# Two small table stores per batch, issued by ScalarE instead of SyncE

## The chip, the cores and the metric

The kernel runs on one core of one Trainium2 chip. A core has five engines with an instruction queue each: TensorE (PE, matmuls), VectorE (DVE), ScalarE (ACT), GpSimd (POOL) and SyncE (SP, which here does nothing but issue transfers). All work through their queues in order and wait for each other by semaphores. Transfers between the on-chip memory and HBM run on 16 DMA engines; here SP issues nearly all of them, POOL the indexed ones, and ACT three tiny ones at the start. The metric is device time in microseconds: the median of several runs. A profile is one further execution.

## The reference

Two layers of a graph network on `x` of 32 batches x 512 channels x 1024 nodes, each with a residual and a layer norm:

```python
# layer 0, per batch
q = einsum('c,cn->n', wq, x);  k = einsum('c,cn->n', wk, x)
scores = leaky_relu(q[None, :] + k[:, None], 0.01)
att = softmax(scores, axis=-1)
agg = einsum('cn,mn->cm', x, att)
x = layernorm(x + relu(einsum('oc,cm->om', adj, agg) + bm[:, None]), axis=-1)
# layer 1, per batch
x = layernorm(x + einsum('nf,nm->mf', x, adj * adj) + bias, axis=-1)
```

Layer 0's weight is `adj`, layer 1's `support * kernel` with both equal to `adj`.

## The kernel before

**Attention without the 1024 x 1024 matrix.** A score depends on q[n] + k[m] alone, and leaky ReLU has two branches, so exp(score) is a product of a factor in n and a factor in m on either side of a threshold. With the nodes sorted by q, the sum over n for a given m is a prefix sum with one factor plus a suffix sum with the other. For each batch the kernel therefore

- projects x to rows of 512 values and an attention column (`project`, L338, PE; `keep`, L357 and L359, DVE and ACT copies out of PSUM);
- ranks the nodes by q (`place`, L403, DVE) and counts for each m how many lie under its threshold (`count`, L428, ACT, after `line`, L395, has copied q);
- scatters the rows to a table in HBM in order of rank (`send`, L415, POOL), and fetches them back sorted into nine blocks `zs` (`fetch`, L461 and L466, SP);
- makes the table of prefix and suffix sums in nine steps (below);
- gathers for each m its rows of the table (`pick`, L543, POOL), scales and adds them (`scale`, `gain`, L582 and L587), transposes (`turn`, L596) and normalises: `add` L603 on DVE, `square` L611 and L612 on ACT, `root0` L619 and L620 on POOL, `finish` L627 and L628 on ACT.

Layer 1 follows with seven half-size products instead of eight (`multiply`, L676, on PE, out of `y`), `read` (L699, L697), statistics, `apply` (L729) and `store` (L734).

**A table step.** Step k (0 to 8) handles block 8 - k from one end (the suffix sums, i = 0) and block k from the other (the prefix sums, i = 1):

- `t{k}`: eight matmuls on PE with triangular weights (L510), four for each block;
- `e{k}`: ACT copies both results out of PSUM (L522); from step 4 on they overwrite blocks of `zs`;
- `cp{k}` and `ca{k}`: the last row of each result is carried into the next block (L528), for i = 0 by POOL, for i = 1 by ACT. `t{k+1}` needs both;
- `ts{k}` (`table_store`, L530 to L539): two stores of 60 rows x 2052 bytes (48 rows for the last block) to the table in HBM, i = 0 first.

```python
        for i, j in enumerate(blocks(step)):
            n = RH if j < NB - 1 else TL
            nc.sync.dma_start(
```

Here NB is 9, RH 60 and TL 48. Step 7's second store is of 60 rows, step 8's of 48.

**The order.** It is written out by hand. Three strings of step names say in which order work is issued: `BEGIN` (batches 0 and 1 and what belongs beside them), `SLOT`, which is run 28 times and interleaves four neighbouring batches, and `END`. Every engine gets its instructions in that order. `SLOT` handles the table of batches 2 to 29. Around the last two table steps it reads:

```python
    ... t7 p27 e7 ld2 mx cp7 ts7 k121 qb mr ca7 rt2 en ts4 y1 t8 r0 sA e8 r1
    sB sq3 ts8 m0 sh sd0 ql ld3 T1 m1 c0 sd1 r2 m3 rdp1 pi3 r3 y2 m2 rt3 r4 pi2 y3 m6 ...
```

On ACT this gives `e7`, `k121` (L359), `ca7` (L528), `y1` (L627 and L628), `e8`, `sq3` (L611, L612), `ql` (L395), `c0` (L428), `rdp1` (L699), `y2`, `y3` (L627 and L628 each). `p27`, `mx`, `qb`, `t8` and `m6` are PE's. In `m6` PE reads what `y3` has written. POOL has `sd0` and `sd1` (scatters of the next batch), then `pi3`, the first gather, which waits for all 18 stores of the table, and behind it `rt3`, the root that `y3` needs.

**Transfers and semaphores.** Transfers of SP and ACT share eight semaphores, handed out in turn in the order of the program. A transfer waits, before it is issued, for the landing of the one that had its semaphore before, eight places earlier. For `ts7`'s second store that is `ld0`, a load of 512 KB of x (L131); for `ts8`'s second store it is `ts6`'s first. A store also waits for the copy that wrote its source.

Of the kernel before, what the change touches and what calls it, by code (L numbers as in the profile page):

```python
# [23 lines left out]
def gat_gcn_resnorm_kernel(  # L24
# [11 lines left out]
    nc = tc.nc  # L36
# [13 lines left out]
    NB = N // R + 1  # L50
# [449 lines left out]
    def blocks(step):  # L500
        return NB - 1 - step, step
# [28 lines left out]
    def table_store(b, step):  # L530

        ts = tss[b, step]
        td = tdb[b % 2].rearrange("(s w u) c -> s w u c", w=2, u=3)
        for i, j in enumerate(blocks(step)):
            n = RH if j < NB - 1 else TL
            nc.sync.dma_start(
                out=td[j * RH : j * RH + n, 0, 1 + i, 1:ZW],
                in_=ts[i * G + 1 : i * G + 1 + n, 0 : ZW - 1],
            )  # L539
# [253 lines left out]
    for k in range(NB):  # L793
        also(1, f"t{k}", table, k)
        also(1, f"e{k}", table_out, k)
        if k < NB - 1:
            also(1, f"cp{k}", carry, k, 0, nc.gpsimd)
            also(1, f"ca{k}", carry, k, 1, nc.scalar)
        also(1, f"ts{k}", table_store, k)
# [177 lines left out]
```

## Time and profile before

| | |
|---|---|
| median of 3 runs | 2201.99 us (2200.96 to 2205.12) |
| the profiled execution | 2198.41 us, span 2196.7 us |
| PE, DVE, ACT, POOL busy | 96%, 81%, 75%, 45% of the span |
| mean granted clock of TensorE | 0.990 |
| stores of L536 | 576 of 120 KB or 96 KB, all issued by SP |
| one period of `SLOT` | about 65 us |

In a line of the order of time the first number is the start in us from the span's start, the second the length; a bracket names idle time of the engine before it and what ended it. In a line of busy time by stage the columns are the stretch and its length in us, then busy time and number of instructions of PE, PE's weight loads, DVE, ACT and POOL, the clock, the share of the DMA engines' time and GB/s. Issues of transfers stand under SPq or ACTq with the time that the queue took to issue them; what the engine itself does meanwhile is not shown by that line. PE's busy time is that of pipelined matmuls, whose ends are modelled.

### The profile page before, as it was taken

Reading aid. Unit: us, or ns where it says so; the run is one execution under the profiler, and the core shown is the slowest. Engines: PE = TensorE matmul, PEld = TensorE weight load, DVE = VectorE, ACT = ScalarE, POOL = GpSimd, SP = SyncE. Lnnn points to the kernel's source line nnn. Section 1 sums busy time; section 2 is a strip of 40 time slices with the busy share of each in tenths; the row PEclk is TensorE's granted clock in tenths of the full one; section 3 lists DMA queues with packets and bytes.
Section 4 is the critical chain, followed back from the end, with each engine's and each line's share of the span. In section 5 each row is a group of like instructions: output and inputs, shape, how many; then the busy total and the mean of one; then the engine's idle time right before and its main releaser. Section 6 shows DMA issues by size and latency. Waiting matters only on the chain.

```text
span 2196.7 us, 35479 instructions
## 1 busy us (share of the span) xinstructions
PE 2102.5 (96%) x11697; PEld 1222.4 (56%) x11697; DVE 1775.9 (81%) x3576; ACT 1652.8 (75%) x2758; POOL 987.6 (45%) x1291
## 2 busy tenths in 40 slices
PE   7879999999999999999999999999999999999877
PEld 5446555556555556555656555556655556655433
DVE  7567888888888888888888898888888888888666
ACT  1577777887777887777888777878777788777765
POOL 1344455444445444445443445544445544445442
PEclk9999999999999999999999999999999999999998
DMA  7567888878888777888777889887888887888752
GB/s 250 166 229 252 264 266 281 257 239 254 268 260 277 262 247 244 268 246 286 266 250 234 265 253 282 273 249 233 262 265 267 282 252 236 258 265 264 221 205 96
DMA packets 179152, 548.86 MB, mean 250 GB/s; under 512 B 27404, under 2 KB 27416, under 8 KB 178968
## 3 DMA queue, kind: packets, MB, share of 16 engines
q1 hardware_dynamic: 121600, 277.06, 43.7%
q0 software_dynamic: 57344, 269.52, 34.3%
q8 instruction: 93, 1.52, 0.3%
q14 instruction: 91, 0.75, 0.1%
q10 hardware_dynamic: 24, 0.01, 0.0%
HBM read 338.17 MB, written 208.30 MB: 249 GB/s over the span
## 4 chain that ended last, share of the span: by engine, by line
PE 62%; ACT 12%; DVE 10%; issue 6%; DMA 6%; POOL 3%; SPq 1%; DVEq 0%; POOLq 0%; ACTq 0%
PE zp_A L338 18%; PE tp L510 10%; PE oA L676 9%; PE zp_B L338 8%; PE op L596 5%; PE zp_C L338 4%; DVE junk L403 4%; ACT y L628 4%; PE oB L676 3%; PE oC L676 3%; DMA zs<-td 2%; ACT rows L582 2%; ACT v L699 1%; POOL zs L528 1%; DMA td<-zs 1%
## 5 line engine op out<-in xcount | busy, mean ns | idle before, releaser
L587 DVE SCALAR_TENSOR_TENSOR rows<-rows,ra 128x512 f32<-128x512 f32 x512 | 366.2, 739 | 20.9 <-ACT rows L582 17.6
L676 PE MATMUL oA<-y,adj_sb 128*128 128x512 f32 x768 | 356.6, 607 | 9.8 <-ACT y L628 6.3
L415 POOL DMA_INDIRECT td<-zrow,ranki x256 | 269.3, 1052 | 213.7 <-DVE idx L439 80.0
L510 PE MATMUL tp<-zs,lq 128*64 128x257 f32 x2304 | 335.1, 392 | 27.2 <-POOL zs L528 16.3
L543 POOL DMA_INDIRECT rows<-td,idx x256 | 297.1, 1160 | 88.1 <-issue 68.0
L403 DVE SCALAR_TENSOR_TENSOR junk<-qb,zrow,first 128x1024 int8<-128x1024 f32 x240 | 307.1, 1279 | 10.9 <-PE qb L376 4.2
L528 POOL COPY zs<-ts 1x513 f32<-1x513 f32 x128 | 93.2, 728 | 474.4 <-ACT ts L522 474.3
L338 PE MATMUL zp_A<-wb,x 128*64 128x257 f32 (+1 forms) x1536 | 278.9, 388 | 12.6 <-issue 3.5
L428 ACT ACTIVATE junk<-lq,kc 128x1024 int8<-128x1024 f32 x240 | 274.4, 1143 | 2.0
L603 DVE SCALAR_TENSOR_TENSOR y<-op,nbm,x 128x1024 f32<-128x1024 f32 x128 | 163.8, 1282 | 127.4 <-PE op L596 127.2
L676 PEld LDWEIGHTS oA<-y,adj_sb 128*128 128x128 f32 x768 | 144.7, 193 | 191.7 <-issue 153.8
L510 PEld LDWEIGHTS tp<-zs,lq 128*64 128x64 f32 x2304 | 168.7, 136 | 135.6 <-POOL zs L528 37.8
L582 ACT ACTIVATE rows<-rows,ra 128x512 f32<-128x512 f32 x256 | 180.1, 718 | 77.5 <-DVE den L574 39.5
L359 ACT COPY zrow<-zp_A 128x514 f32<-128x514 f32 x192 | 112.8, 588 | 147.4 <-PE zp_A L338 130.1
L338 PEld LDWEIGHTS zp_A<-wb,x 128*64 128x64 f32 (+1 forms) x1536 | 177.0, 155 | 77.3 <-issue 25.1
L528 POOL COPY zs<-zs 1x513 f32<-1x513 f32 x128 | 78.3, 611 | 253.0 <-ACT zs L522 253.0
L628 ACT ACTIVATE y<-y,nb,r 128x1024 f32<-128x1024 f32 x128 | 158.9, 1241 | 4.3
L705 DVE BATCH_NORM_STATS2 st<-v 128x6 f32<-128x512 f32 x240 | 151.9, 674 | 0.0
L612 ACT ACTIVATE x<-y,nm 128x1024 f32<-128x1024 f32 x128 | 147.2, 1150 | 4.2
L729 ACT ACTIVATE v<-v,nb,rs 128x1024 f32<-128x1024 f32 x120 | 148.1, 1234 | 2.3 <-DVE nb L721 1.4
L596 PE MATMUL op<-ident,rows 128*128 128x128 f32 x1024 | 141.2, 282 | 4.6 <-DVE rows L587 2.6
L596 PEld LDWEIGHTS op<-ident,rows 128*128 128x128 f32 x1024 | 114.9, 143 | 46.1 <-issue 24.6
(162 smaller groups left out, 3784.6 us busy)
## 6 DMA issues: line engine op xcount, KB each, us to landing
x<-in_x_dram SPq DMA_DIRECT2D x128, 512.0 KB
out_dram<-v SPq DMA_DIRECT2D x120, 512.0 KB
zs<-td SPq DMA_DIRECT2D x64, 602.3 KB
td<-zs SPq DMA_DIRECT2D x288, 120.2 KB
td<-ts SPq DMA_DIRECT2D x224, 120.2 KB
zs<-td SPq DMA_DIRECT2D x64, 240.9 KB
zs<-td SPq DMA_DIRECT2D x96, 120.5 KB
td<-zs SPq DMA_DIRECT2D x8, 514.0 KB
```

The costliest lines, as they stand in the source:

```text
L338: nc.tensor.matmul(zp[n : n + wide, m, 0:CE], side(b, g, a)[:, c, m * P + n : m * P + n + wide], wb[:, w, c, :], start=first and c == 0, s ...
L403: nc.vector.scalar_tensor_tensor(junk(b)[:, 0:N], qbs[b], zrow[:, nt, 0:1], first[:, o : o + N], ALU.subtract, ALU.is_lt, accum_out=rank[: ...
L415: sc = nc.gpsimd.indirect_dma_start(out=td[:, :], out_offset=bass.IndirectOffsetOnAxis(ap=ranki[:, nt : nt + 1], axis=0), in_=zrow[:, nt, ...
L428: nc.scalar.activation(junk(b)[:, N : 2 * N], qs[b], AF.Sign, bias=kcs[b][:, nt : nt + 1], accum_out=signs(b)[:, nt : nt + 1],)
L510: nc.tensor.matmul(tp[i * G : (i + 1) * G, h, 0:CE], lw[:, ks[i], :], zs[:, j, 1 + h * CE : 1 + (h + 1) * CE], start=True, stop=True,)
L528: copy(zs[row : row + 1, to, 1:ZW], ts[row : row + 1, 0 : ZW - 1])
L543: nc.gpsimd.indirect_dma_start(out=rows[:, mt, :], out_offset=None, in_=tdb[b % 2].rearrange("(s u) c -> s (u c)", u=3), in_offset=bass.In ...
L582: nc.scalar.activation(u, u, AF.Copy, scale=ratios(b)[:, k, 1:2])
L587: nc.vector.scalar_tensor_tensor(u, rg[:, k, i, 1 : C + 1], ratios(b)[:, k, i : i + 1], u, ALU.mult, ALU.add)
L596: nc.tensor.transpose(op[:, mt * P : (mt + 1) * P], rg[:, mt, 1, 1 + ot * P : 1 + (ot + 1) * P], ident)
L628: nc.scalar.activation(yall[:, ot], yall[:, ot], AF.Identity, bias=nb, scale=r)
L676: nc.tensor.matmul(o[:, m, :], quarters[w][:, a, m * P : (m + 1) * P], part(b, y)[:, a, :], start=fresh and a == 0, stop=a == CT // 2 - 1, ...
```

## The change

In steps 7 and 8 (NB - 2 and NB - 1) of every batch, the second store (i = 1) is put into ACT's instruction queue instead of SP's. It stands there at the place where `SLOT`, `BEGIN` or `END` names `ts7` or `ts8`: in `SLOT` between `e7` and `k121`, and between `sq3` and `ql`. The first store of both steps, and all stores of steps 0 to 6, stay on SP. These are 64 of the 576 stores. What is stored, where to, and which semaphore it has are as before.

```diff
@@ table_store
         for i, j in enumerate(blocks(step)):
             n = RH if j < NB - 1 else TL
-            nc.sync.dma_start(
+            by = nc.scalar if i and step >= NB - 2 else nc.sync
+            by.dma_start(
                 out=td[j * RH : j * RH + n, 0, 1 + i, 1:ZW],
                 in_=ts[i * G + 1 : i * G + 1 + n, 0 : ZW - 1],
             )
```

## The prediction

> **What bounds the kernel now.** I read the page's busy table first, then one steady stretch by stages, then the instructions of ACT and PE around the change in order of time, and the waits last.
>
> The page's first part:
>
> ```profile
> PE 2102.5 (96%) x11697; PEld 1222.4 (56%) x11697; DVE 1775.9 (81%) x3576; ACT 1652.8 (75%) x2758; POOL 987.6 (45%) x1291
> ```
>
> PE has 4% to lose, ACT 25%. But shares are means. The busy time by stage, in one batch's period and in the part of it around the change (columns: stretch, length, busy us of each engine with its instructions, clock, DMA share, GB/s):
>
> ```profile
> 1127.30:1142.70 15.40, 15.35 (x75) 8.47 (x71) 12.04 (x29) 15.00 (x25) 7.81 (x12) 1.00 0.79 240
> 1142.70:1192.20 49.50, 48.24 (x282) 30.27 (x282) 41.98 (x81) 35.40 (x62) 21.80 (x28) 1.00 0.81 262
> 1076.70:1141.60 64.90, 64.42 (x366) 37.48 (x365) 54.41 (x111) 51.42 (x87) 30.60 (x41) 1.00 0.80 261
> ```
>
> The last row is a whole period: 64.9 us, PE idle 0.5 of it. The first row is the 15.4 us in which both touched stores lie: there ACT is as full as PE (15.00 and 15.35 of 15.40). So in this stage ACT has no slack of its own, and the question is whether what follows it on PE has some. ACT in order of time, from step 7's copy out of PSUM to the layer norm's last tile (start, length, instruction):
>
> ```profile
> 1131.41 0.57 ACT L522 COPY zs<-tp 128x514 f32<-128x514 f32 x1
> 1132.04 0.59 ACT L359 COPY zrow<-zp_A 128x514 f32<-128x514 f32 x1
> 1132.65 0.61 ACT L528 COPY zs<-zs 1x513 f32<-1x513 f32 x1
> 1133.30 0.29 ACT L627 ACTIVATE nb<-nm,r 128x1 f32<-128x1 f32 x1
> 1133.62 1.24 ACT L628 ACTIVATE y<-y,nb,r 128x1024 f32<-128x1024 f32 x1
> 1134.77 0.57 ACT L522 COPY zs<-tp 128x514 f32<-128x514 f32 x1
> 1135.24 0.20 ACT L611 ACTIVATE nm<-sm 128x1 f32<-128x1 f32 x1
> 1135.47 1.15 ACT L612 ACTIVATE x<-y,nm 128x1024 f32<-128x1024 f32 x1
> 1136.52 0.19 ACT L612 ACTIVATION_READ_ACCUMULATOR x<-y,nm 128x1 f32 x1
> 1136.62 0.99 ACT L395 COPY lq<-qb 128x1024 f32<-128x1024 f32 x1
> ...
> 1141.46 1.24 ACT L628 ACTIVATE y<-y,nb,r 128x1024 f32<-128x1024 f32 x1
> ```
>
> The two L522 copies are `e7` and `e8`, L528 is ACT's carry `ca7`, the last L628 is `y3`. No gap is longer than 0.07 us. PE in the same stretch:
>
> ```profile
> 1130.87 1.14 PE L338 MATMUL zp_A<-wb,x 128*64 128x257 f32 x8
> 1131.94 0.32 PE L383 MATMUL mx<-ident,q 128*128 128x128 f32 x1
> 1132.10 1.04 PE L376 MATMUL qb<-ident,zrow 128*128 128x128 f32 x8
> 1133.06 1.34 PE L510 MATMUL tp<-zs,lq 128*64 128x257 f32 x8
> ```
>
> `t8` (the last line) takes 1.34 us where the eight matmuls of steps 6 and 7 take 1.09 and 1.19: its second block is loaded at 1133.32, just after `ca7` ends at 1133.27. So PE already waits for ACT inside `t8`. It does so again at `y3`: PE's first gap in each period, 0.10 us before L676, ends with ACT L628. In this stage ACT's lateness is PE's lateness, one for one.
>
> **The change part by part.** Per batch one store of 120 KB (`ts7`) and one of 96 KB (`ts8`), 64 in all, go from SP's queue to ACT's, each in its old place of the program order. No bytes, no waits' targets and no compute instructions change. The order of ACT's and SP's remaining instructions is the same.
>
> *Off SP.* Two issues of about 0.4 us fewer per batch (in the trace the touched store of `ts7` takes 0.397 on SP, that of `ts8` 0.390). `ts4`, which stands behind `ts7`, is issued 0.4 us sooner; `ts8`'s first store still waits for `e8`, the load after it for ACT's L612, and the fetch behind that waits some 24 us for POOL's scatters. Nobody waits for `ts4` before `ts8` has landed. Gain: nothing; its cover is SP's own waiting, 766 us over 31 fetches.
>
> *`ts7`'s second store on ACT.* It stands between `e7` and L359. It needs `e7` complete, so ACT's sequencer, which otherwise hands L359 over while `e7` runs, first waits for `e7`'s end, then issues, then hands on L359. From the rows: SP starts the twin 0.026 us after `e7`'s end; after an issue 0.11 us pass until the next instruction starts (0.052 to the next entry, 0.017 for its wait, 0.04 to the start, as SP's and ACT's queue entries show). With an issue of length D, L359 starts 0.136 + D after `e7`; it starts 0.066 after now, as it does in all 28 batches (2 to 29) that use the repeating plan. Added: D + 0.07.
>
> D on ACT for a 60-row store is not in the trace. Lower bounds: ACT's two undisturbed issues, four rows each, 0.259 and 0.313 us. SP's 60-row issue takes 0.314 at least, 0.355 as `ts7`'s first store and 0.397 behind that. Upper: both stores are released by the same event, so ACT's may wait out SP's: 0.355 + 0.397 = 0.75. ACT's only issue that started together with one of SP's is the first of these lines:
>
> ```profile
> L76 ACTq DMA_DIRECT2D v<-in_L_gnn_wq_dram x1: 567/567/567, 0.8 to 0.8; - x1
> L76 ACTq DMA_DIRECT2D v<-in_L_gnn_wk_dram x1: 259/259/259, 1.4 to 1.4; - x1
> L76 ACTq DMA_DIRECT2D v<-in_L_gnn_bm_dram x1: 313/313/313, 1.7 to 1.7; - x1
> ```
>
> It took 0.567 against 0.26 to 0.31 for its like, with SP's 0.43 us issue begun 6 ns later. I take D = 0.48, midway between SP's 0.397 and this 0.567: 0.55 us per batch.
>
> A row and a rule on this: the 0.567 row says that two issuers at once cost one of them some 0.28 us. The Trainium skill (Perfetto Trace Analysis, DMA Instruction — HWDGE) says more: the descriptor generator is locked for one issuer until its descriptors are made, and the time spent on that lock is inside the profiled issue. If ACT lost that lock every time the sum would be that of the second rival below, if it won it that of D = 0.31; the row lies between.
>
> All that follows on ACT moves by 0.55: L359, `ca7`, so `t8` on PE, then `y1`, `e8`, and everything to `y3`. PE idles 0.55 in `t8`, so at `y3` its gap stays 0.1. There is no second charge, and no refund: the rest of the period has 0.4 us of PE gaps that other waits set. The store's wait for the transfer eight places earlier (a load of x) never bites: by the landings in the trace it is down 1.6 to 3.2 us before `e7` ends, in all 28 batches.
>
> *`ts8`'s second store on ACT.* It stands between L612's accumulator read and L395. L611 and L612 have already waited for `e8`; the transfer eight places earlier landed 1.8 us or more before `e8` ended. ACT's sequencer runs ahead of the engine: its two wait entries for L428, which stand behind L395, are done at 1135.9 and 1136.17 while L612 runs until 1136.62. So the issue lies under L612's 1.15 us with some 0.4 us to spare. Cost 0; if ACT did not run ahead past it, D, 0.26 to 0.48.
>
> *First and last batches* (0, 1, 30, 31): there the plan has `ca7` (0.61 us) or L428 (1.15 us) ahead of the moved issue, which covers it; in batch 31 the pair of `ts8` may land 0.4 us sooner and a gather with it. Counted as 0.
>
> *Sum:* 28 x 0.55 = 15.4 us. The profiled execution took 2198.41 us (span 2196.70); with the sum 2213.8. The three timed runs have a median of 2201.99, 3.6 above it; on that the sum gives 2217.4, and I say 2217.
>
> **The rivals.**
>
> *ACT issues at no cost* (the sequencer gives the transfer away and goes on): L359 is then late by 0.07 + 0.03 at most, 28 x 0.1 = 2.8 us, 2202 to 2205. Against it: on SP an issue holds the next entry back for its whole 0.3 to 0.4 us, and ACT's three at the start follow each other in the same way. 11%.
>
> *ACT always waits out SP's twin:* D = 0.75, 28 x 0.82 = 23 us, 2225. For it, the simultaneous release and the 0.567 row; against it, that row is only 0.28 above its like. 15%.
>
> *Both stores are exposed:* 28 x (0.55 + 0.48) = 29 us, 2231. Against it, the sequencer's run-ahead. 6%.
>
> *Faster.* In four batches ACT's `y3` waits for POOL's reciprocal root, and PE with it:
>
> ```profile
> 617.91 0.29 ACT L627 ACTIVATE nb<-nm,r 128x1 f32<-128x1 f32 x1 [0.67 <-POOL r L620]
> ```
>
> That root stands on POOL behind the first gather, which waits for the last landing of `ts8`; there it came 3.0 to 3.5 us after issue instead of 2.1. On a queue of its own the second store may land sooner. All four gaps gone give 0.78 + 1.12 + 0.60 + 0.90 = 3.4 us, 2198.6. It decides only if the added time per batch is under 3.4/28 = 0.12 us, that is D under 0.05, a fifth of the shortest issue in the trace. 3%.
>
> **How the numbers follow.** Forecast (D from 0.26 to 0.6: 28 x 0.33 to 0.67, 2211 to 2221) 65%; the rivals 11, 15, 6 and 3%. The range takes in D = 0.75 with 1 to 3 us for issues that stall (SP's touched and twin stores lost 2 us in four such) and reaches below D = 0.26 for an issue partly hidden: 2206 to 2228, with about 19% outside. A run of this kernel can tell some 0.2%, 4.4 us, from no change. Slower: 65 + 15 + 6 = 86%; within: 11%; faster: 3%.
>
> **What would show it.** Right: on ACT an issue of 0.3 to 0.75 us after each `e7`, L359 0.5 to 0.7 us after `e7`'s end, `t8` on PE some 0.5 us longer, the period 65.5 instead of 64.94, and L395 still close behind L612. Wrong: L359 still at 0.07 (the issue was free); a gap before L395 (the second store is exposed); `t8` longer but the period not (PE had slack that I did not see).

## The result, and the profile after

On one chip, six runs each, the changed kernel took 2216.9 us (median; 2213.51 to 2218.63) and the kernel before 2202.53 us (2200.03 to 2208.59). The ratio is 1.0062, with a 95% interval of 1.0049 to 1.0076: slower by some 14 us, as forecast (2217.0, between 2206 and 2228). That the total came within 0.1 us is luck: the main term was put too high, and a wait that the prediction had ruled out made up for it.

The profiled execution took 2216.41 us (span 2214.7), 18.0 more than that of before, at the same mean granted clock (0.989 against 0.990). From here on line numbers above 536 are one higher than before, since the diff adds a line: L537 is the store, L613 was L612, L629 was L628, L677 was L676. The page's busy line:

```profile
PE 2114.6 (95%) x11697; PEld 1226.9 (55%) x11697; DVE 1780.0 (80%) x3576; ACT 1653.8 (75%) x2758; POOL 983.8 (44%) x1291
```

ACT's 2758 instructions are no busier than before (1653.8 against 1652.8): issuing a transfer does not count as busy. PE's busy time grew by 12.1 us with the same number of matmuls: the added wait lies inside `t8`, where the records of the matmuls ahead of it (0.38 to 0.43 us each, with modelled ends) reach over it, so that most of it counts as busy. Busy time by stage shows the same (columns as before: stretch, length, busy us of PE, weight loads, DVE, ACT, POOL, clock, DMA share, GB/s):

```profile
1139.00:1154.40 15.40, 15.37 (x73) 8.24 (x69) 11.87 (x29) 14.29 (x24) 7.36 (x11) 1.00 0.81 243
1089.00:1154.40 65.40, 64.91 (x366) 37.51 (x365) 54.51 (x110) 51.19 (x87) 30.43 (x40) 1.00 0.83 257
```

The first row is the stage of the two stores. ACT is 14.29 us busy of 15.40, where it was 15.00: it now stands still for 0.7 us more there, in a stage in which it sets the pace. The second row is the period, 65.4 us instead of 64.9, with the same 0.5 us in which PE is idle.

ACT in order of time, in the batch shown of before (ACTq is its queue, here issuing a store):

```profile
1142.85 0.57 ACT L522 COPY zs<-tp 128x514 f32<-128x514 f32 x1
1143.44 0.36 ACTq L537 DMA_DIRECT2D td<-zs  x1
1143.90 0.59 ACT L359 COPY zrow<-zp_A 128x514 f32<-128x514 f32 x1 [0.48 <-PE mx L383]
1144.51 0.61 ACT L528 COPY zs<-zs 1x513 f32<-1x513 f32 x1
1145.15 0.29 ACT L628 ACTIVATE nb<-nm,r 128x1 f32<-128x1 f32 x1
1145.48 1.24 ACT L629 ACTIVATE y<-y,nb,r 128x1024 f32<-128x1024 f32 x1
1146.62 0.57 ACT L522 COPY zs<-tp 128x514 f32<-128x514 f32 x1
1147.09 0.20 ACT L612 ACTIVATE nm<-sm 128x1 f32<-128x1 f32 x1
1147.33 1.15 ACT L613 ACTIVATE x<-y,nm 128x1024 f32<-128x1024 f32 x1
1147.33 0.31 ACTq L537 DMA_DIRECT2D td<-zs  x1
1148.38 0.18 ACT L613 ACTIVATION_READ_ACCUMULATOR x<-y,nm 128x1 f32 x1
1148.47 0.99 ACT L395 COPY lq<-qb 128x1024 f32<-128x1024 f32 x1
```

Between `e7` and L359 there is now an issue and a hole of 0.48 us; before, L359 started 0.07 us after `e7`. The profile puts the hole down to PE's `mx`, which had long been done: what ended it was the issue. The second issue lies under L613, and L395 follows as closely as before. On PE the hole is in `t8`, which took 1.34 us before:

```profile
1144.50 1.76 PE L510 MATMUL tp<-zs,lq 128*64 128x257 f32 x8
```

All of ACT's 64 issues as a group (least, median, greatest in ns):

```profile
L537 ACTq DMA_DIRECT2D td<-zs x64: 313/322/367, 97.6 to 2132.3; - x64
```

Those of `ts7` take 0.358 us (in 28 of 32 batches), those of `ts8` 0.31. Over the 28 batches of `SLOT` the time from the end of `e7` to the end of `e8` has a median of 3.780 us, before 3.361: 0.419 more. That is 0.030 until the issue starts, 0.358 for it, 0.097 until L359 starts, less the 0.066 of before. `t8` grew by 0.418 (1.343 to 1.761), and the shortest period from 64.94 to 65.33. So 28 x 0.419 = 11.7 us of the 18.0.

The rest begins on SP. Its issues in the same batch, before the first fence, after the second:

```profile
1135.36 0.32 SPq L536 DMA_DIRECT2D td<-zs  x1
```

```profile
1143.44 0.36 SPq L537 DMA_DIRECT2D td<-zs  x1
1148.43 0.31 SPq L537 DMA_DIRECT2D td<-zs  x1
```

The line of before is `ts8`'s first store, issued 0.03 us after `e8` (its end is 1135.34). After, the first line is `ts7`'s first store and the second `ts8`'s: it starts 1.24 us after `e8`, which ends at 1147.19 (the median of the 28 batches is 0.95). What SP waited for, summed over the run (us in total, times, longest), is a line that the view of before does not have:

```profile
SPq L537 <- DMA td<-zs: 88.2, 28, 3.7
```

A store waits for the landing of a store: its semaphore is still held. The eight semaphores go round in the order in which the compiled program lists the transfers, and the semaphore that each transfer has in the traces shows that this order differs with one store on another engine. Before, it was `ts6`'s pair, `ld2`, `ts7`'s pair, `ts4`'s pair, `ts8`'s pair. After, `ts7`'s second store is listed first, ahead of `ts6`'s pair, and `ts8`'s second between the two of `ts4`. Eight places ahead of `ts8`'s first store now stands `ts7`'s second, which lands only 4 to 5 us after `e7`. (The sentence "which semaphore it has are as before", in the description of the change above, is wrong, and so is the prediction's statement that no wait's target changes.)

The last landing of `ts8` after `e8` went from a median of 2.50 us to 3.00, and POOL, which waits with its first gather for it, does the root for `y3` later. Four batches waited for that root before; now it is more (all waits of ACT for it: 15 times, 9.9 us, against 6 times, 8.3 us). In this batch:

```profile
1153.41 0.29 ACT L628 ACTIVATE nb<-nm,r 128x1 f32<-128x1 f32 x1 [0.31 <-POOL r L621]
```

and PE, a moment later, stands still for `y3`:

```profile
1155.03 1.55 PE L677 MATMUL oC<-y,adj_sb 128*128 128x512 f32 x3 [0.52 <-ACT y L629]
```

Beyond the 0.1 us that PE always waited here, these gaps came to 3.9 us before and 7.1 after in the 27 periods from `t8` of batch 2 to `t8` of batch 29. The account of the two profiled executions: these periods grew by 14.3 us (1764.4 to 1778.7), of which 10.6 is PE's longer time in `t8`, 3.2 the gaps at `y3`, and the rest small waits; the period ahead of them (`t8` of batch 1 to `t8` of batch 2) grew by 2.1 (66.7 to 68.7); what lies ahead of that by 0.8; the end by 0.8. In that one period PE has two waits that it did not have before, 0.33 us for ACT's L629 and 0.81 for DVE's L357. It is longer in all five profiles with both second stores on ACT (68.2 to 69.4 us) than in the seven others (66.7 to 67.9), so part of it goes with the stores; by what path is not shown. The profiled execution of before was also 4.1 us under its median, that of after 0.5.

### The profile page after: what moved, and what is told of

Its sections match the earlier page's. It is cut to its first block, busy times and chain, and to the rows that moved or that the text cites. A ratio compares the mean times of both kernels' runs of the same rounds, so it can differ in the third digit from the quotient of the medians.

```text
span 2214.7 us, 35509 instructions
## 1 busy us (share of the span) xinstructions
PE 2114.6 (95%) x11697; PEld 1226.9 (55%) x11697; DVE 1780.0 (80%) x3576; ACT 1653.8 (75%) x2758; POOL 983.8 (44%) x1291
## 4 chain that ended last, share of the span: by engine, by line
PE 55%; ACT 14%; DVE 12%; DMA 6%; issue 6%; POOL 4%; SPq 1%; ACTq 0%; DVEq 0%; POOLq 0%
PE zp_A L338 14%; PE oA L677 10%; PE tp L510 9%; PE zp_B L338 8%; DVE junk L403 5%; PE zp_C L338 4%; PE op L597 4%; ACT y L629 4%; PE oB L677 3%; DMA zs<-td 3%; PE oC L677 3%; ACT x L613 2%; DMA td<-zrow,ranki 2%; POOL rows L544 2%; ACT zs L522 2%
## 5 line engine op out<-in xcount | busy, mean ns | idle before, releaser
L510 PE MATMUL tp<-zs,lq 128*64 128x257 f32 x2304 | 349.8, 395 | 28.3 <-POOL zs L528 14.6
L677 PE MATMUL oA<-y,adj_sb 128*128 128x512 f32 x768 | 356.3, 606 | 9.5 <-ACT y L629 4.4
L428 ACT ACTIVATE junk<-lq,kc 128x1024 int8<-128x1024 f32 x240 | 274.4, 1143 | 2.0
L677 PEld LDWEIGHTS oA<-y,adj_sb 128*128 128x128 f32 x768 | 144.4, 192 | 191.6 <-issue 157.9
L359 ACT COPY zrow<-zp_A 128x514 f32<-128x514 f32 x192 | 112.7, 587 | 156.4 <-PE zp_A L338 130.6
L629 ACT ACTIVATE y<-y,nb,r 128x1024 f32<-128x1024 f32 x128 | 158.8, 1241 | 4.3
L613 ACT ACTIVATE x<-y,nm 128x1024 f32<-128x1024 f32 x128 | 147.1, 1150 | 4.1
```

Source lines behind the costliest of these rows:

```text
L428: nc.scalar.activation(junk(b)[:, N : 2 * N], qs[b], AF.Sign, bias=kcs[b][:, nt : nt + 1], accum_out=signs(b)[:, nt : nt + 1],)
L510: nc.tensor.matmul(tp[i * G : (i + 1) * G, h, 0:CE], lw[:, ks[i], :], zs[:, j, 1 + h * CE : 1 + (h + 1) * CE], start=True, stop=True,)
L613: nc.scalar.activation(xs[b][:, ot], yall[:, ot], AF.Square, bias=nm, accum_out=sq)
L629: nc.scalar.activation(yall[:, ot], yall[:, ot], AF.Identity, bias=nb, scale=r)
L677: nc.tensor.matmul(o[:, m, :], quarters[w][:, a, m * P : (m + 1) * P], part(b, y)[:, a, :], start=fresh and a == 0, stop=a == CT // 2 - 1, ...
```

## The experiments

The theory: an issue placed between two copies on ACT holds ACT's next copy back by its own length, since it waits for the first copy to end (0.42 us per batch, through `t8` to PE); the other issue is free; and the new wait on a semaphore adds a few us at `y3`. Rivals: the second store of `ts8` costs, too; the transfers themselves, on a second queue, get in each other's way; or the issue is long only because SP issues at the same moment. Each ratio is the one on record, against runs of the kernel before on the same chip; it can differ from that of the two medians (most in the last pair, 0.9951 against 0.9932).

**One store at a time.** Only `ts7`'s second store on ACT:

```diff
-            by = nc.scalar if i and step >= NB - 2 else nc.sync
+            by = nc.scalar if i and step == NB - 2 else nc.sync
```

> Only step 7's second store is issued by ACT; step 8's is back on SP. Theory A (the cost is ACT's issue behind e7: 0.42 us from wait, issue and hand-over in each of 28 batches, and beside it step 8's store on SP that now waits for the semaphore of the ACT store): 11 to 12 us from the issue and 1 to 4 us from the late store, so 2214 to 2218 us; L359 again 0.48 us after e7. Rival B (each issue on ACT costs, wherever it stands): half of the whole change, about 7 us, 2209 to 2211.

Measured: 2219.99 us against 2200.67, ratio 1.0094 (1.0076 to 1.0112), above the 2214 to 2218 expected. In the trace L359 starts 0.485 us after `e7` and `e7` to `e8` takes 3.780 us, as with both stores.

```profile
1143.07 0.36 ACTq L537 DMA_DIRECT2D td<-zs  x1
1143.53 0.59 ACT L359 COPY zrow<-zp_A 128x514 f32<-128x514 f32 x1 [0.49 <-PE mx L383]
1144.13 1.76 PE L510 MATMUL tp<-zs,lq 128*64 128x257 f32 x8
```

`ts8`'s second store, back on SP, is now the one that waits for `ts7`'s semaphore: it is issued 0.92 us after `e8` (median; 0.38 before), the last landing comes at 3.04, and the waits for the root sum to 6.8 us in the 28 batches (3.0 before, 4.8 with both). So this store alone makes the whole loss and more. Its ratio is 0.3% above that of the change. The two profiled spans differ by 0.7 us only (2215.4, 2214.7): the 27 periods are 3.3 us longer than with both stores moved, 1.9 of them in the gaps at `y3`, and the period ahead of them is 1.8 shorter. The rest of the difference, between two chips, stays open.

Only `ts8`'s second store on ACT:

```diff
-            by = nc.scalar if i and step >= NB - 2 else nc.sync
+            by = nc.scalar if i and step == NB - 1 else nc.sync
```

> Only step 8's second store is issued by ACT, under the 1.15 us of L612. Theory A: nothing on ACT (L395 starts as before), no store of step 8 waits for a semaphore that lands late; 2200 to 2204 us, if anything a little below before, since the second store is issued 0.25 us sooner. Rival B (each issue on ACT costs): about +7 us, 2209 to 2211. Rival C (a second queue makes the landings slower): step 8's stores land later than 2.5 us after e8 and y3 waits for POOL's root, +2 to +5 us.

Measured: 2203.59 us, ratio 1.0012 (0.9996 to 1.0027). `e7` to `e8` is 3.361 us and L395 starts 1.281 after `e8`, both as before. On ACT the issue under L613 is free:

```profile
1139.20 1.15 ACT L613 ACTIVATE x<-y,nm 128x1024 f32<-128x1024 f32 x1
1139.20 0.31 ACTq L537 DMA_DIRECT2D td<-zs  x1
1140.25 0.18 ACT L613 ACTIVATION_READ_ACCUMULATOR x<-y,nm 128x1 f32 x1
1140.35 0.99 ACT L395 COPY lq<-qb 128x1024 f32<-128x1024 f32 x1
```

There is nothing to gain from it either: the second store was issued 0.14 us after `e8` instead of 0.38, but the pair's last landing came at 2.65 us, before at 2.50. A queue of its own did not bring the bytes down sooner. Rival C is not excluded by this run alone: the waits for the root sum to 4.9 us in its 28 batches (3.0 before), and the interval leaves up to 0.27%. The next run, with the same two queues, speaks against it: there they sum to 2.5.

**The same two stores, one place later.** `ts7`'s second store behind L359 instead of ahead of it (`tu7` issues step 7's first store, `tv7` its second); `ts8` as in the change:

```diff
-    ts7 k121 qb mr ca7 rt2 en ts4 y1 t8 r0 sA e8 r1 sB sq3 ts8 ...
+    tu7 k121 tv7 qb mr ca7 rt2 en ts4 y1 t8 r0 sA e8 r1 sB sq3 ts8 ...
```

> Both second stores on ACT as in the changed kernel, but in the 28 repeated batches step 7's stands behind L359 (k121) instead of ahead of it. By then e7 is done, so the issue can lie under L359's 0.59 us. Step 8's first store then follows an SP store on its semaphore. Theory A: L359 at 0.07 us after e7 again, carry L528 at its old place, period 64.9 us; 2200 to 2205 us. Rivals B and C (the issue costs wherever it stands, or the second queue does): the loss stays, 2214 to 2218.

Measured: 2204.09 us, ratio 1.0018 (1.0003 to 1.0032); the loss of 0.6% shrank to 0.2%. In order of time:

```profile
1135.18 0.57 ACT L522 COPY zs<-tp 128x514 f32<-128x514 f32 x1
1135.81 0.59 ACT L359 COPY zrow<-zp_A 128x514 f32<-128x514 f32 x1
1135.87 0.32 ACTq L539 DMA_DIRECT2D td<-zs  x1
1136.42 0.61 ACT L528 COPY zs<-zs 1x513 f32<-1x513 f32 x1
```

By the time the issue has waited for `e7`, L359 has been handed to the engine, and the issue lies under it. L359 starts at 0.067 again, `t8` takes 1.343, `e7` to `e8` 3.361, the shortest period is 64.92, and the 27 periods sum to 1764.4, as before. Bytes, queues and engines are those of the change. So the loss in `t8` comes neither from the second queue nor from the transfers: it is the place of the issue in ACT's order, and the cost is the issue together with the wait for the copy just ahead. The order of the semaphores is another here, too: `ts8`'s first store is issued 0.025 us after `e8` again. So this run takes away both parts of the loss at once; the stretch from `e7` to `e8`, above, and the next pair of runs tell them apart. Of the 0.2% that is left, the profile shows 1.8 us in the period ahead of the 27.

**The root ahead of the gather.** To take away the path over POOL, `rt3` was put ahead of `pi3` in `SLOT`, in the kernel before and in the changed one:

```diff
-    rdp1 pi3 r3 y2 m2 rt3 r4 pi2 y3 m6 ...
+    rdp1 rt3 pi3 r3 y2 m2 r4 pi2 y3 m6 ...
```

> The kernel before, with POOL's root for the last tile (rt3, L619 and L620) ahead of the first gather (pi3) in the repeated plan, so that y3 no longer stands behind the landing of step 8's stores. Theory A: y3's waits of 0.5 to 1 us in four batches (3.4 us in the profile of before) go; 2197 to 2200 us. Rival: the gather, about 1 us later, holds up what reads it; 2203 to 2230.

> The changed kernel with POOL's root for the last tile ahead of the first gather, so that step 8's late store no longer reaches y3. Theory A: what is left against the kernel before with the same reordering (2198.6 us) is the issue alone, 28 x 0.42 = 11.7 us: 2209 to 2212 us, with no wait of y3 for POOL. Rival: if the late store costs by other ways as well (the gathers and what reads them), 2214 to 2218 as without the reordering.

Measured: in the kernel before 2198.6 us, ratio 0.9991 (0.9979 to 1.0004); in the changed one 2210.04, ratio 1.0034 (1.002 to 1.0047). ACT's wait for the root ahead of `y3` is gone in all 28 batches of both. The change still shows `e7` to `e8` of 3.781 and a shortest period of 65.35, but the distance between the two ratios is 0.43% here, some 9.5 us, instead of 0.62%, some 14. So the issue is the larger part, and the semaphore's wait, through the root, some 4 us; the three intervals, about 0.13% on either side each, leave that between nothing and some 9, and the profiles put it at 3.2 (between profiles of kernels without the late store the same gaps differ, too: 3.5 to 5.8 us in all). Of the kernel before alone the edit makes nothing that can be told from no change: its first gather comes 1.28 us later.

**A second dose.** Both stores of step 7 on ACT, those of step 8 on SP, root first:

```diff
-            by = nc.scalar if i and step >= NB - 2 else nc.sync
+            by = nc.scalar if step == NB - 2 else nc.sync
```

> A double dose: both stores of step 7 on ACT behind e7, those of step 8 on SP, and POOL's root first as in the run beside it. Theory A: L359 about 0.9 us after e7 (0.03 + two issues of 0.36 to 0.40 + 0.1), so a second 0.4 us per period: 2220 to 2225 us. Rival (most of the loss is one wait for e7 and not the issue): as the single dose, 2209 to 2213.

Measured: 2221.46 us, ratio 1.0082 (1.0065 to 1.0099). L359 starts 0.920 us after `e7`, `e7` to `e8` takes 4.215: another 0.435 for the second issue, and the shortest period goes to 65.78, another 0.43.

```profile
1079.26 0.57 ACT L522 COPY zs<-tp 128x514 f32<-128x514 f32 x1
1079.85 0.79 ACTq L537 DMA_DIRECT2D td<-zs  x2
1080.74 0.59 ACT L359 COPY zrow<-zp_A 128x514 f32<-128x514 f32 x1 [0.92 <-DVE bw L390]
1082.03 1.08 PE L510 MATMUL tp<-zs,lq 128*64 128x257 f32 x6 [0.47 <-ACT zs L528]
```

The cost goes with the number of issues on ACT, one dose each. In the batch shown they took 0.335 and 0.418 us while SP issued `ts4`'s stores beside them in 0.421 and 0.408; SP took 0.426 and 0.449 for those in the kernel before (medians), with no other issue beside them. So SP was not made slower by ACT's issues.

Whether the issue is long because SP starts its own at the same moment can be read from the change itself. In 28 of the 32 batches the two issues of `ts7` start within 0.02 us of each other, and ACT's takes 0.357 to 0.362 us. In the other four it takes 0.321 or 0.322; in one of these, batch 21, SP's comes 0.30 us later, and L359 starts 0.447 us after `e7` instead of 0.485. So the simultaneous start makes up 0.04 of the 0.42 us, no more.

**Slack for ACT, first try.** If PE is slow here because ACT is late, giving ACT slack should cover the issue. `ca7` was put ahead of L359 and `c0` (L428, 1.15 us) behind `y3`, root first, in the kernel before and in the changed one:

```diff
-    ts7 k121 qb mr ca7 rt2 en ...      T1 m1 c0 sd1 r2 m3
-    rdp1 pi3 r3 y2 m2 rt3 r4 pi2 y3 m6 ...
+    ts7 ca7 k121 qb mr rt2 en ...      T1 m1 sd1 r2 m3
+    rdp1 rt3 pi3 r3 y2 m2 r4 pi2 y3 c0 m6 ...
```

> The kernel before with slack made on ACT, no store moved: carry ca7 ahead of k121, the count c0 (1.15 us) behind y3, POOL's root first. If ACT's fullness from e7 to y3 is what PE waits for, t8's wait for ca7 (0.25 us) and y3's (0.1 us) go: up to 28 x 0.35 = 10 us, 2189 to 2196. If another wait stands close behind, 2196 to 2203.

> The same three reorderings on the changed kernel, so ACT issues both second stores, step 7's still right behind e7. Theory A (the issue costs only because ACT has no slack there): ca7 ends 0.2 us earlier than in the kernel before although it stands behind the issue, y3 has 0.8 us to spare, and the time is within 4 us of the run beside it. Rival B (an issue costs wherever it stands): 11 us and more above it.

Neither gave the slack that was sought. The kernel before went to 2223.48 us (1.0077; 1.0054 to 1.01), the changed one to 2232.22 (1.0134; 1.0115 to 1.0153), 8.7 above it by the medians, some 12 by the ratios. The first fits neither of its two expectations; the second lies between its two by the medians, and in its rival's range by the ratios. ACT's `y3` does end sooner (6.78 us after `e8` instead of 7.37). But PE now waits for DVE in each period, 0.40 us in the first and 0.78 in the second:

```profile
1086.13 3.70 PE L676 MATMUL oB<-rows,ws 128*128 128x512 f32 x8 [0.40 <-DVE rows L652]
```

```profile
1088.85 3.70 PE L677 MATMUL oB<-rows,ws 128*128 128x512 f32 x8 [0.78 <-DVE rows L653]
```

DVE's `en` needs L359's row, and L652, which makes PE's operand, stands behind `en` in DVE's queue. L359 starts 0.67 us after `e7` now, so DVE is late and PE with it: over the 27 periods PE's waits for DVE, at L652 and at others behind it, grow from 4 to 30 us in the kernel before, while the periods grow by 21.9. Slack given to one reader of ACT was taken from another.

**Slack, second try.** Now no copy is moved back. PE's seed matmuls (`sA`, `sB`, L660), which need nothing of `t8`, stand ahead of it, so that PE has work while `ca7` ends; `c0` is behind `y3` and the root first, as in the last try:

```diff
-    ... y1 t8 r0 sA e8 r1 sB sq3 ts8 m0 sh sd0 ql ld3 T1 m1 c0 sd1 r2 m3
-    rdp1 pi3 r3 y2 m2 rt3 r4 pi2 y3 m6 ...
+    ... y1 sA sB t8 r0 e8 r1 sq3 ts8 m0 sh sd0 ql ld3 T1 m1 sd1 r2 m3
+    rdp1 rt3 pi3 r3 y2 m2 r4 pi2 y3 c0 m6 ...
```

> The kernel before with three changes of order and no change of work: the seed matmuls of layer 1 (PE, L660) stand ahead of t8 instead of behind it, ACT's c0 (L428) stands behind y3, and the root that y3 needs stands ahead of the first gather on POOL. PE then has 0.3 to 0.8 us of other work while ca7 ends, so the 0.25 us that t8 waits now and the 0.10 us at y3 should go, and no copy that DVE waits for is moved back (that undid the last try). Theory (PE follows ACT in this stage and nothing else is near): 28 x 0.1 to 0.35 us and some 3 us for the root, 4 to 12 us under the kernel before, 2190 to 2198. Rival (another engine is as close to the bound, as DVE was in the last try): PE's gaps appear elsewhere and the time is 2199 or more.

> The same three changes of order in the changed kernel. Theory (the issue costs ACT 0.42 us per batch, and PE only what its slack does not cover): L359 still 0.485 us after e7's end, but of 28 x 0.42 = 11.7 us a part is covered; 0 to 8 us above the run before this one. Rival (the loss does not come through t8 and y3 but through DVE, whose queue waits for L359's row): the full 11 us or more above it, with PE's waits on DVE.

The kernel before with this order took 2188.81 us (2183.25 to 2195.47), ratio 0.9951 (0.9933 to 0.9968): faster than both kernels of the case. PE's wait inside `t8` is gone, in all 28 batches:

```profile
1127.98 0.39 PE L660 MATMUL oA<-seeds,ones 3*128 3x512 bf16 x2
1127.99 0.39 PE L660 MATMUL oB<-seeds,ones 3*128 3x512 bf16 x2
1128.30 1.09 PE L510 MATMUL tp<-zs,lq 128*64 128x257 f32 x8
```

1.09 us is what the matmuls take unhindered; the shortest period is 64.44 instead of 64.94, and the gap at `y3` no longer occurs. Three edits were made together, so what each gave is not told apart, but the 0.25 us in `t8` and 0.10 at `y3` are 0.35 of the 0.50.

The changed kernel with the same order took 2201.14 us, ratio 0.9987 (0.9975 to 1.0): 12.3 above by the medians, 8 by the ratios. Here the cover was expected to save part of the loss; by the medians the time went to the rival, by the ratios it is at the end of the theory's range. The rival's cause did not come: PE's gaps ahead of the products that read DVE's rows are no larger. It is `t8` again:

```profile
1134.49 0.39 PE L661 MATMUL oA<-seeds,ones 3*128 3x512 bf16 x2 [0.24 <-ACT zrow L359]
1134.50 0.39 PE L661 MATMUL oB<-seeds,ones 3*128 3x512 bf16 x2
1134.82 1.40 PE L510 MATMUL tp<-zs,lq 128*64 128x257 f32 x8
```

`t8` has a median of 1.397, 0.31 over 1.089, in each batch, and in four of them the seeds wait for L359, too, as in this one. Of 0.42 us only 0.11 were covered; the shortest period grew by 0.34 (64.44 to 64.78), and the 27 periods together by 12.0 us, 9.2 of them by this. The other 2.8 lie in waits scattered over single slots and are not explained.

## Why the prediction was right, point by point

**What bounds the kernel** was right. In this stage PE follows ACT one for one: 0.419 more on ACT made 0.418 more in `t8` and 0.40 more in the period. Moving the issue by one copy took all three away. (L359 started 0.066 us after `e7` in 27 of the 28 batches, not in all: in one it started 0.05 before `e7`'s end. Nothing hangs on it.)

**`ts7`'s second store: the mechanism was right, its length too long.** The sum was D + 0.07 with D = 0.48. Measured: D = 0.358 and the rest 0.061. So the term is 11.7 us instead of 15.4. D was taken midway between SP's 0.397 and the 0.567 of ACT's one issue at the start that had begun together with one of SP's, and that row was read as contention worth 0.28 us. The contention here is far smaller: SP's and ACT's issues begin 4 ns apart (1143.439 and 1143.443 in the batch shown), and they take 0.356 and 0.358 us; SP's first store of `ts7` took 0.355 before, alone, and ACT's takes 0.321 where SP's does not start with it. The nearest row was the twin store itself, of the same shape, and would have given 0.355. What made the first issue of the program 0.567 is open.

With that the rule drawn on in the prediction is weighed, too. The Trainium skill (Perfetto Trace Analysis, DMA Instruction — HWDGE) has the descriptor generator locked for one issuer, with the wait for the lock inside the profiled issue. Between SP and ACT the trace shows no wait as long as an issue: of two that start together, SP's is as long as alone (0.356 against 0.355) and ACT's is 0.04 us longer (0.358 against 0.321). If that is the lock, the wait for it is 0.04 us long and not an issue; the runs do not show whether it is. The rival with the full wait (D = 0.75, 2225 us) did not come, in any of the 28 pairs that start within 0.02 us of each other.

**`ts8`'s second store costs nothing**: right on ACT, with the reason given, shown by L395 at 1.28 us after `e8` as before. The run with that store alone agrees (1.0012, its interval holding 1), though it could hide up to 0.27%.

**SP's side** was counted as nothing, on the ground that `ts8`'s first store still waits for `e8` alone and that the semaphores eight places earlier are long free. This step failed. The check was made for the two moved stores, with the old order of transfers; the order itself changed, and an unmoved store came to wait for a moved one. It costs 3.2 us at `y3` by the profiles, some 4 by the runs with the root ahead of the gather. The path is the one named for the rival "faster", the last landing of `ts8`, POOL's gather and the root; it went the other way.

**The sum** was so 15.4 for one term, where 11.7 for the issue, 3.2 at `y3` and some 3 that are not explained, mostly ahead of the 27 periods, came in the profiled execution (18.0). By the medians the change costs 14.4. Right in total by luck, with two errors of opposite sign.

**The rivals**: a free issue is excluded (L359 at 0.485); two exposed issues as well. "Faster" had no ground: a second queue did not land the store sooner (2.65 against 2.50 us).

## What to carry to other kernels

Before a transfer is moved to a compute engine's queue, look at what stands on either side of it there: behind the copy that it must wait for, it holds the engine for a whole issue and two handovers (0.42 us here); one instruction further on it was covered. Then list which transfer has which semaphore in the new order, since an unmoved transfer can inherit a semaphore that is still held. And where PE waits for a copy in each period, other matmuls put ahead of it may be worth trying before the copying engine is relieved (0.5% here, together with two other changes of order).

## What the runs showed that was not expected

- Issues on SP and ACT run beside each other almost without lengthening. The issue of 60 rows on ACT took 0.358 us where SP's started within 0.02 us of it, and 0.32 otherwise, also when SP's was already running (under L359); SP's took 0.356 beside ACT's and 0.355 alone. That of 48 rows under L613 took 0.31.
- L359 behind an issue starts 0.097 us after the issue's end; without one it starts 0.066 us after the end of the copy ahead.
- Of `ts8`'s two stores (120 and 96 KB), on two queues and issued 0.12 us apart, the later landed 2.65 us after `e8`; on one queue and 0.36 us apart, 2.50.
- In a few batches the copy behind the issue starts 0.28 us later than in the others: with the change in one of 28 (0.376 us after the issue's end instead of 0.097), in the second dose in three (batches 8, 16 and 24; 0.376 to 0.391). Why is open.
